# A graph layer with routed experts on one core: edge sums split into two single products, earlier residuals and routing, denser expert blocks

## The chip, the core and the metric

The kernel runs on one core of a Trainium2 chip. The core has five engines that each work through their own list of instructions in order: TensorE (PE in the profile, its weight loads PEld), VectorE (DVE), ScalarE (ACT), GpSimd (POOL) and SyncE (SP, which here only issues transfers). They wait for each other by semaphores, and transfers go through 16 DMA engines. The metric is the device time of one execution in microseconds. Eleven runs of the kernel before gave a median of 1468.36 us (1464.17 to 1476.13).

## What is computed

A layer over 6250 nodes of 256 values (x) and 100000 edges (src, dst, weight), with dst sorted. In short:

```python
xn = layernorm(x)
h = xn @ W;  deg = segment_sum(edge_weight, dst) + 1;  dinv = rsqrt(deg)
agg = segment_sum(dinv[src] * edge_weight * dinv[dst] * h[src], dst) + dinv**2 * h
g = relu(0.5 * (layernorm(agg + b) * gamma + beta) + 0.5 * xn)
q, k = elu(xn @ Wq.T) + 1, elu(xn @ Wk.T) + 1;  v = xn @ Wv.T        # 8 heads of 32
x1 = x + g + (q @ (k.T @ v) / max(q . k.sum, 1e-6)) @ Wproj.T + bproj
y = layernorm(x1);  logits = y @ gate_w + gate_b                      # 16 experts, the best 2
moe = sum over the best 2 of softmax weight * (relu(y @ w1[e] + b1[e]) @ w2[e] + b2[e])
out = x1 + layernorm(y + moe) * gamma2 + beta2
```

## The kernel before, in words

Nodes lie in 49 tiles of 128 rows (X stays in SBUF). Edges lie in 782 chunks of 128; eight chunks form a group g, and a group's destinations lie in a window of 128 rows at steps of 64, so that two or three groups fill a tile.

**Setup** (to about 100 us): edge lists are transposed into columns (`columns`), degrees are summed on TensorE from one-hot factors that VectorE builds (L448, L452, L460), the row statistics are taken, and the table `w_hs` of rows dinv * xn is written to DRAM from Q, seven tiles at a time (`table`, L519 to L531).

**Main loop** (L1300): a slot is one chunk. In slot c GpSimd gathers the chunk's 128 table rows from DRAM into one of 12 row buffers (L1306), and VectorE builds a 128x128 matrix `hot` of edge weights at the edges' destinations (L1310). LAG = 6 slots later TensorE multiplies hot by the rows in float32 and adds into the group's accumulator (L1319); each such product is recorded as two matmuls. A finished group is scaled and added to its tile's sum `agg` (L1331). PE, DVE, ACT and SP execute exactly the order in which the program is written; GpSimd's instructions alone are placed by the scheduler.

Everything else is woven into slots by `Weave`: a piece of work is a generator that is put at a slot, and each `yield n` lets n slots go by. `attend` (a tile each 3.6 slots up to slot 157) makes queries into Q and the attention's sums. `residual` (two tiles at a time, at slot 16 * t1 + 4 + LAG + 3 or later, ten slots apart) turns sums into x1, takes its statistics, normalises it on ScalarE (L745), transposes and copies it, and multiplies by gate_w (L754) for the logits, 22 slots in all. For each of eleven phases of tiles (PHASES: up to tile 8, 12, 16, ... 40, 46, 49) `route` comes RES = 24 slots behind the last residual; it takes the best two experts and gives each token a place in blocks of 128 tokens of one expert (slot_i, L906). `scatter` normalises the phase's tiles on ScalarE (L994) into four places and writes the rows by GpSimd to `w_xslots` (L1005); a fifth tile's activation waits until a scatter has left its place. `expert` loads a block's weights (about 1.1 MB) and tokens by SP, four blocks deep, and needs TensorE for two transposes (L1076), w1 (L1087) and w2 (L1098). Blocks stand seven slots apart, six in the phase that ends at tile 40, four behind that or near the end. `combine` gathers each token's two results (L1145) and writes the output.

The transfers that clear w_xslots and w_yslots (1 MB each) stand on SP's queue: 11 during setup, 23 from slot 4 on.

The slots of interest: phase 9 (tiles 40 to 45) is routed at slot 773; the last two residuals start at 781 and 791; the last phase is routed at 815; 78 of 114 blocks start at or before slot 782; block 88, the first of the last phase, starts at 829.

## Time and profile before

| what | value |
|---|---|
| median of 11 runs | 1468.36 us |
| profiled execution: time, span | 1469.18 us, 1467.4 us |
| mean granted TensorE clock | 0.936 |
| first and last gather of the main loop start | 104.5 us, 1207.4 us |
| first transposes of block 88 | 1289.7 us |
| first and last gather of combine start | 1291.2 us, 1447.9 us |

A line of the profile's groups gives the source line, engine, operation, what it writes and reads, the count, then busy time in us and mean ns of one, then the idle time of the engine just before and what ended most of it. A line of the timeline gives start, duration, engine, line and operation, with idle time and releaser in brackets. A line of the stretches gives the stretch, its length, then for PE, PEld, DVE, ACT and POOL the busy us (and number of instructions), then the granted clock, the DMA engines' share and GB/s. A stretch's DMA share and an engine's busy time are of that stretch alone, so they say more than the shares of the whole span.

### The profile page before, as it was taken

The numbers are of one execution on the slowest core, as the hardware profiler recorded it, in microseconds if no ns is written. First come the engines' busy times: TensorE is split into PE (matmuls) and PEld (weight loads), VectorE is DVE, ScalarE is ACT, GpSimd is POOL, SyncE is SP. The second block draws the span as 40 slices with busy tenths as digits, with TensorE's granted clock in tenths as the row PEclk, the third lists the DMA queues.
The fourth block names the chain that finished last, engine by engine and source line by source line (L and its number), as shares of the span: only waits on it lengthen the run. The fifth ranks groups of instructions, "written<-read, shape, count | busy, mean of one in ns | idle before, by whom it ended". The sixth has DMA issues, their size and how long they took to land. (4 is left out here: it accounts for less than half of the span.)

```text
span 1467.4 us, 24332 instructions
## 1 busy us (share of the span) xinstructions
PE 1230.8 (84%) x6923; PEld 994.8 (68%) x6923; DVE 953.9 (65%) x3302; ACT 500.6 (34%) x1354; POOL 961.2 (66%) x999
## 2 busy tenths in 40 slices
PE   4879999978777788979889798798988997968890
PEld 3846666646655677868678687686877886857770
DVE  7954454458877484756847568375684666568885
ACT  3763444422322222313223232232332233434551
POOL 1017777777767777777777777777777773167643
PEclk9999999999967999999999999898998998989995
DMA  8979943333335777778768687786767886989993
GB/s 257 317 261 371 382 134 102 105 104 113 110 104 168 230 251 265 254 232 265 266 230 299 228 261 244 259 270 224 268 212 267 294 290 219 314 291 385 376 325 93
DMA packets 176921, 353.83 MB, mean 241 GB/s; under 512 B 26769, under 2 KB 116020, under 8 KB 176770
## 3 DMA queue, kind: packets, MB, share of 16 engines
q1 hardware_dynamic: 128790, 223.10, 44.1%
q0 software_dynamic: 47712, 128.17, 27.6%
q8 instruction: 61, 1.00, 0.3%
q10 hardware_dynamic: 268, 0.82, 0.2%
q14 instruction: 90, 0.74, 0.2%
HBM read 277.60 MB, written 74.38 MB: 240 GB/s over the span
## 5 line engine op out<-in xcount | busy, mean ns | idle before, releaser
L1306 POOL DMA_INDIRECT rows<-w_hs,src_t x782 | 754.7, 965 | 329.2 <-issue 92.3
L1319 PE MATMUL acc<-rows,hot 128*128 128x256 f32 x1564 | 446.3, 401 | 91.4 <-DMA rows<-w_hs,src_t 78.9
L1310 DVE TENSOR_SCALAR hot<-iota_g,loc_t,w_t 128x128 f32<-128x128 f32 x782 | 268.6, 361 | 285.0 <-PE acc L1319 278.7
L1319 PEld LDWEIGHTS acc<-rows,hot 128*128 128x128 f32 x1564 | 278.3, 198 | 168.4 <-issue 72.4
L1005 POOL DMA_INDIRECT w_xslots<-Q,slot_i x98 | 100.5, 1025 | 80.5 <-ACT Q L1081 41.0
L1098 PE MATMUL yp<-early,hT 128*128 128x256 f32 x592 | 144.5, 388 | 1.0 <-ACT hT L1094 0.8
L1145 POOL DMA_INDIRECT Q<-w_yslots,slot_i x98 | 100.1, 1021 | 66.1 <-DVE xn L1161 22.9
L1094 ACT ACTIVATE hT<-hp,early 128x128 f32<-128x128 f32 x296 | 84.3, 368 | 149.9 <-PE hp L1087 115.3
L1087 PE MATMUL hp<-Q,early 128*128 128x128 f32 x992 | 125.3, 281 | 8.0 <-ACT Q L1081 8.0
L1087 PEld LDWEIGHTS hp<-Q,early 128*128 128x128 f32 x992 | 122.1, 196 | 13.3 <-ACT Q L1081 10.3
L1098 PEld LDWEIGHTS yp<-early,hT 128*128 128x128 f32 x592 | 114.0, 196 | 18.0 <-ACT hT L1094 2.2
L1081 ACT COPY Q<-xtp 128x256 f32<-128x256 f32 x114 | 42.2, 370 | 225.5 <-PE xtp L1076 223.2
L1087 PE MATMUL hp<-Q 128*128 128x128 f32 x832 | 111.3, 291 | 8.8 <-ACT Q L1081 8.8
L1087 PEld LDWEIGHTS hp<-Q 128*128 128x128 f32 x832 | 108.1, 206 | 13.6 <-ACT Q L1081 11.4
L576 PE MATMUL kq<-early,xnT 128*128 128x512 f32 (+1 forms) x196 | 94.5, 605 | 4.1 <-ACT xnT L572 4.1
L324 ACT ACTIVATE sd<-mv,eps_t 128x2 f32<-128x2 f32 (+2 forms) x76 | 22.6, 298 | 217.9 <-DVE mv L320 212.2
L1098 PE MATMUL yp<-Q,hT 128*128 128x256 f32 x320 | 79.8, 394 | 2.3 <-ACT hT L1094 2.2
L706 PE MATMUL hp<-w_sb,two_a 128*128 128x256 f32 (+1 forms) x196 | 58.1, 449 | 19.7 <-ACT two_a L678 19.7
L1098 PEld LDWEIGHTS yp<-Q,hT 128*128 128x128 f32 x320 | 61.4, 198 | 12.7 <-ACT hT L1094 4.5
L1331 DVE SCALAR_TENSOR_TENSOR agg<-acc,dinv,agg 64x256 f32<-64x256 f32 x135 | 64.9, 481 | 2.8
L706 PEld LDWEIGHTS hp<-w_sb,two_a 128*128 128x128 f32 (+1 forms) x196 | 42.4, 223 | 30.5 <-ACT two_a L678 22.0
L1094 ACT ACTIVATE hT<-hp,Q 128x128 f32<-128x128 f32 x160 | 45.4, 368 | 45.9 <-PE hp L1087 35.5
(306 smaller groups left out, 1727.6 us busy)
## 6 DMA issues: line engine op xcount, KB each, us to landing
early<-in_experts SPq DMA_DIRECT2D x61, 642.0 KB
early<-in_experts SPq DMA_DIRECT2D x62, 512.0 KB
Q<-in_experts SPq DMA_DIRECT2D x52, 512.0 KB
Q<-in_experts SPq DMA_DIRECT2D x27, 642.0 KB
w_xslots<-zero_b SPq DMA_DIRECT2D x16, 1024.0 KB
w_yslots<-zero_b SPq DMA_DIRECT2D x16, 1024.0 KB
Q<-w_xslots SPq DMA_DIRECT2D x114, 128.0 KB
w_yslots<-Q SPq DMA_DIRECT2D x114, 128.0 KB
```

The lines of the kernel that those rows point to most:

```text
L576: nc.tensor.matmul(kq[:r], xnT[:, k, :r], wkq[:, k, :], start=(k == 0), stop=(k == 1))
L706: nc.tensor.matmul(hp[:r0, i, :], agT[:, k, i * P:i * P + r0], w_sb[:, k, :], start=(k == 0), stop=(k == 1))
L1005: i = nc.gpsimd.indirect_dma_start(out=xslots, out_offset=IndirectOffsetOnAxis(ap=slot_i[:r, t, k:k + 1], axis=0), in_=y[:r], in_offset=No ...
L1081: nc.scalar.copy(xT, tp[:, :2, :])
L1087: nc.tensor.matmul(hp[:, f, :], w1[:, c, f * P:(f + 1) * P], xT[:, c, :], start=(c == 0), stop=(c == 1))
L1094: act(hT[:, f, :], hp[:, f, :], AF.Relu, bias=b1[:, f:f + 1], scale=1.0)
L1098: nc.tensor.matmul(yp[:, :D], hT[:, f, :], w2[:, f, :], start=(f == 0), stop=(f == FJ - 1 and not as_row))
L1145: g = nc.gpsimd.indirect_dma_start(out=got[i, k]()[:r], out_offset=None, in_=yslots, in_offset=IndirectOffsetOnAxis(ap=slot_i[:r, t, k:k + ...
L1306: nc.gpsimd.indirect_dma_start(out=hrows[c], out_offset=None, in_=hs, in_offset=IndirectOffsetOnAxis(ap=src_t[:, c:c + 1], axis=0))
L1310: v.tensor_scalar(hots[c], iota_g[:, group_of(c) % 2, :], loc_t[:, c:c + 1], w_t[:, c:c + 1], op0=OP.is_equal, op1=OP.mult)
L1319: nc.tensor.matmul(accs[g], hots.pop(c), hrows.pop(c), start=begin, stop=end)
L1331: v.scalar_tensor_tensor(agg(t)[p0:p1], acc[p0:p1, :], dinv[p0:p1, t:t + 1], agg(t)[p0:p1], op0=OP.mult, op1=OP.add)
```

## The change

It consists of six parts that go together.

- The sums of 420 of the 782 chunks (groups below 24, and the odd ones from 40 on: `in_parts`) no longer multiply float32 by float32. `hot` becomes a matrix of zeros and ones (VectorE compares two chunks at once), ScalarE writes row times weight into a float32r tile `high` three slots behind the gather, VectorE writes the rest of the product into `low` one slot later, and TensorE multiplies hot by high and by low, seven slots behind the gather. The other chunks keep their float32 product, six slots behind.
- The gate's product takes the transposed x1 itself; mean and deviation come in afterwards, by the column sums of gate_w (`gsum`, made once) and two small VectorE operations. The two activations of L745 and five slots fall away.
- Residuals start at 16 * t1 + 4 + LAG - 1 with LAG = 7, three slots earlier than before; routing follows 19 slots behind and not 24. Phase 9 is routed at slot 765, the last residuals start at 778 and 788, the last phase is routed at 807, block 88 starts at 821, and 81 blocks start at or before slot 782.
- The blocks of the phase that ends at tile 40 stand five slots apart.
- Gathered rows have a ring of 15 buffers of their own, high and low five each; behind the main loop a tile `late` takes that memory. To make room Q holds 36 tiles and not 49: the last tiles of the table are staged over earlier ones, and the queries of tiles 36 to 48 go to DRAM and come back eight slots before they are used. The list of sources is turned into columns before the branch on `flag`.
- The 23 transfers that clear memory during the main loop are issued by ScalarE instead of SP.

In the built order of instructions all 18 scatters of the last two phases stand behind the last gather on GpSimd, before as after, and a gather waits for as many semaphores as before (one of them VectorE's or TensorE's).

```diff
+FR = mybir.dt.float32r
...
-LAG = 6
+LAG = 7
+SPLIT = 3
+QT = 36
+RING_ROWS, RING_PARTS = 15, 5
...
-RES = 24
+RES = 19
...
+def in_parts(g):
...
+    return g < 24 or (g >= 40 and g % 2 == 1)
...
-    rows3 = top.tile([P, 3, EW], F32, name="rows3")
-    loc_e, src_e, ew_e = rows3[:ER, 0, :], rows3[:ER, 1, :].bitcast(I32), rows3[:ER, 2, :]
...
+    src_t = top.tile([P, NCA], I32, name="src_t")
...
+        rows3 = cp.tile([P, 3, EW], F32, name="rows3")
+        loc_e, src_e, ew_e = rows3[:ER, 0, :], rows3[:ER, 1, :].bitcast(I32), rows3[:ER, 2, :]
...
+        sf = cp.tile([ER, EW], F32, name="sf")
+        nc.scalar.copy(sf, src_e)
+        columns(nc, cps, ident, sf, src_t)
...
-        windowed_layer(tc, X, rows3, ident, loc_t, w_t, **rest)
+        windowed_layer(tc, X, ident, loc_t, w_t, src_t, **rest)
...
+    w_q = dram.tile([(NT - QT) * P, D], F32, name="w_q")
...
-    def fill(a, first, end):
+    def fill(eng, a, first, end):
...
-            nc.sync.dma_start(a[s * P:(s + q) * P, :].rearrange("(p q) c -> p q c", q=q),
-                              zero[:, None, :].to_broadcast([P, q, D]))
+            eng.dma_start(a[s * P:(s + q) * P, :].rearrange("(p q) c -> p q c", q=q),
+                          zero[:, None, :].to_broadcast([P, q, D]))
...
-    for _ in fill(xslots, 0, SOON):
+    for _ in fill(nc.sync, xslots, 0, SOON):
...
-                sf = sp.tile([ER, EW], F32, name="sf")
-                nc.scalar.copy(sf, src_e)
-                columns(nc, sps, ident, sf, src_t)
...
-    Q = sums.tile([P, NT, D], F32, name="Q")
+    Q = sums.tile([P, QT, D], F32, name="Q")
...
+    staged = [t if t < 5 * TG else t - 4 * TG for t in range(NT)]
...
-        r = rows(t)
+        r, j = rows(t), staged[t]
...
-            act(Q[:r, t, :], X[:r, t, :], AF.Identity, bias=nmr[:r, t:t + 1], scale=rsd[:r, t:t + 1])
+            act(Q[:r, j, :], X[:r, t, :], AF.Identity, bias=nmr[:r, t:t + 1], scale=rsd[:r, t:t + 1])
...
-            v.tensor_scalar(Q[:r, t, :], X[:r, t, :], mv1[:r, t, 0:1], rsd[:r, t:t + 1],
+            v.tensor_scalar(Q[:r, j, :], X[:r, t, :], mv1[:r, t, 0:1], rsd[:r, t:t + 1],
...
-            nc.sync.dma_start(hs[t0 * P:(t0 + n) * P, :].rearrange("(t p) c -> p t c", p=P), Q[:, t0:t0 + n, :])
+            j = staged[t0]
+            nc.sync.dma_start(hs[t0 * P:(t0 + n) * P, :].rearrange("(t p) c -> p t c", p=P), Q[:, j:j + n, :])
...
-                nc.sync.dma_start(hs[NFULL * P:, :], Q[:rows(NFULL), NFULL, :])
+                nc.sync.dma_start(hs[NFULL * P:, :], Q[:rows(NFULL), j + n, :])
...
+    gsum = wp.tile([P, NE], F32, name="gsum")
...
-        v.scalar_tensor_tensor(Q[:r, t, :], e[:r, 1, :], 1.0, pos[:r, 1, :], op0=OP.min, op1=OP.add)
+        q = Q[:, t, :] if t < QT else mp.tile([P, 2, D], F32, name="h2", bufs=2)[:, 0, :]
+        v.scalar_tensor_tensor(q[:r], e[:r, 1, :], 1.0, pos[:r, 1, :], op0=OP.min, op1=OP.add)
...
+        if t >= QT:
+            nc.sync.dma_start(w_q[(t - QT) * P:(t - QT) * P + r, :], q[:r])
...
+        gs = bank("gs")
+        for k in range(2):
+            nc.tensor.matmul(gs[:, :NE], ones, gw[:, k, :], start=(k == 0), stop=(k == 1))
+        v.tensor_copy(gsum, gs[:, :NE])
...
-    def queries(t0):
...
-        return Q[:, t0:min(NT, t0 + 2), :]
...
+    def queries(t0):
...
+        j = t0 if t0 < QT else 9 + (t0 - QT) // 2 % 2 * 2
+        return Q[:, j:j + 2, :]
...
+    def load_queries(ts_):
...
+        for i, t in enumerate(ts_):
+            r = rows(t)
+            nc.sync.dma_start(queries(ts_[0])[:r, i, :], w_q[(t - QT) * P:(t - QT) * P + r, :])
+        return
+        yield
...
-        q = Q[:r0, t0:t1, :]
+        q = queries(t0)[:r0, :n, :]
...
+        tp = turn([X[:r0, t, :] for t in ts_])
...
+        xT = kept(tp, "yT", 1)
...
-        yield 1
-        y = []
+        rest = mp.tile([P, 2, NE], F32, name="rest", bufs=1)
...
-            y.append(mp.tile([P, D], F32, name="row", bufs=3))
-            act(y[i][:r0], X[:r0, t, :], AF.Identity, bias=nm2[:r0, t:t + 1], scale=rs2[:r0, t:t + 1])
-        yield 2
-        tp = turn([a[:r0] for a in y])
-        yield 1
-        yT = kept(tp, "yT", 1)
-        yield 2
+            v.scalar_tensor_tensor(rest[:r0, i, :], gsum[:r0], nm2[:r0, t:t + 1], gb[:r0], op0=OP.mult, op1=OP.add)
+        yield 1
...
-                nc.tensor.matmul(gl[:r0, i, :NE], yT[:, k, i * P:i * P + r0], gw[:, k, :], start=(k == 0), stop=(k == 1))
-        yield 1
-        v.tensor_tensor(logits[:r0, t0:t1, :], gl[:r0, :n, :NE], gb[:r0, None, :].to_broadcast([r0, n, NE]), op=OP.add)
+                nc.tensor.matmul(gl[:r0, i, :NE], xT[:, k, i * P:i * P + r0], gw[:, k, :], start=(k == 0), stop=(k == 1))
+        yield 1
+        for i, t in enumerate(ts_):
+            v.scalar_tensor_tensor(logits[:r0, t, :], gl[:r0, i, :NE], rs2[:r0, t:t + 1], rest[:r0, i, :], op0=OP.mult, op1=OP.add)
...
-    hrow = rows3.rearrange("p a (i d) -> p (a i) d", d=D)
-    NROW = 3 * EW // D
+    NROW = RING_ROWS + 2 * RING_PARTS
+    ringed = ExitStack()
+    rp = ringed.enter_context(tc.tile_pool(name="w_ring", bufs=1))
+    late = []
...
+    def late_row(i):
+        if not late:
+            late.append(msg.enter_context(tc.tile_pool(name="w_late", bufs=1)).tile([P, NROW, D], F32, name="late"))
+        return late[0][:, i, :]
...
+    LATE = 12
...
-        weave.add(fill_at, fill(a, first, MOST + 1))
+        weave.add(fill_at, fill(nc.scalar, a, first, MOST + 1))
...
-            at = max(at, min(NCH, 16 * t1 + 4) + LAG + 3)
+            at = max(at, min(NCH, 16 * t1 + 4) + LAG - 1)
...
+            if t0 >= QT:
+                weave.add(at - 8, load_queries(range(t0, t1)))
...
-            block = max(block + (4 if n > AFTER or block > NCH - 9 else 6 if n == AFTER else 7), ready)
+            block = max(block + (4 if n > AFTER or block > NCH - 9 else 5 if n == AFTER else 7), ready)
...
-    hrows, hots, accs = {}, {}, {}
+    hrows, highs, lows, hots, accs = {}, {}, {}, {}, {}
...
-            hrows[c] = hrow[:, c % NROW, :]
+            hrows[c] = rp.tile([P, D], F32, name="hrow", bufs=RING_ROWS)
...
-            hots[c] = mp.tile([P, P], F32, name="hot", bufs=LAG + 1)
-            v.tensor_scalar(hots[c], iota_g[:, group_of(c) % 2, :], loc_t[:, c:c + 1], w_t[:, c:c + 1],
-                            op0=OP.is_equal, op1=OP.mult)
-        c = slot - LAG
-        if 0 <= c < NCH:
+        c = slot - 3
+        if 0 <= c < NCH and c % 2 == 0:
+            full = [P, 2, P]
+            g = group_of(c)
+            if in_parts(g):
+                hot = mp.tile(full, FR, name="hot", bufs=4)
+                v.tensor_tensor(hot, iota_g[:, g % 2:g % 2 + 1, :].to_broadcast(full),
+                                loc_t[:, c:c + 2, None].to_broadcast(full), op=OP.is_equal)
+            else:
+                hot = mp.tile(full, F32, name="hot", bufs=4)
+                for i in range(2):
+                    v.tensor_scalar(hot[:, i, :], iota_g[:, g % 2, :], loc_t[:, c + i:c + i + 1], w_t[:, c + i:c + i + 1],
+                                    op0=OP.is_equal, op1=OP.mult)
+            hots[c], hots[c + 1] = hot[:, 0, :], hot[:, 1, :]
+        c = slot - SPLIT
+        if 0 <= c < NCH and in_parts(group_of(c)):
+            highs[c] = rp.tile([P, D], FR, name="high", bufs=RING_PARTS)
+            act(highs[c], hrows[c], AF.Identity, scale=w_t[:, c:c + 1])
+        c = slot - SPLIT - 1
+        if 0 <= c < NCH and in_parts(group_of(c)):
+            lows[c] = rp.tile([P, D], FR, name="low", bufs=RING_PARTS)
+            v.scalar_tensor_tensor(lows[c], hrows.pop(c), w_t[:, c:c + 1], highs[c].bitcast(F32), op0=OP.mult, op1=OP.subtract)
+        for c, parts in ((slot - LAG, True), (slot - LAG + 1, False)):
+            if not (0 <= c < NCH and in_parts(group_of(c)) == parts):
+                continue
...
-            nc.tensor.matmul(accs[g], hots.pop(c), hrows.pop(c), start=begin, stop=end)
+            hot = hots.pop(c)
+            if parts:
+                nc.tensor.matmul(accs[g], hot, highs.pop(c), start=begin, stop=False)
+                nc.tensor.matmul(accs[g], hot, lows.pop(c), start=False, stop=end)
+            else:
+                nc.tensor.matmul(accs[g], hot, hrows.pop(c), start=begin, stop=end)
...
+        if slot == NCH + LAG + 1:
+            ringed.close()
```

## The prediction

> **What bounds the kernel now.** I read the busy shares, then busy time by stretch, then GpSimd's instructions in order of time, then the end after the last gather.
>
> ```profile
> PE 1230.8 (84%) x6923; PEld 994.8 (68%) x6923; DVE 953.9 (65%) x3302; ACT 500.6 (34%) x1354; POOL 961.2 (66%) x999
> ...
> L1306 POOL DMA_INDIRECT rows<-w_hs,src_t x782 | 754.7, 965 | 329.2 <-issue 92.3
> L1319 PE MATMUL acc<-rows,hot 128*128 128x256 f32 x1564 | 446.3, 401 | 91.4 <-DMA rows<-w_hs,src_t 78.9
> ```
>
> By these shares TensorE looks like the bound. It isn't, for most of the time. A gather takes 0.95 us, and 0.30 us lies before each, whoever is named as releaser:
>
> ```profile
> 709.64 0.95 POOL L1306 DMA_INDIRECT rows<-w_hs,src_t  x1 [0.30 <-DMA rows<-w_hs,src_t]
> 710.89 1.17 POOL L1306 DMA_INDIRECT rows<-w_hs,src_t  x1 [0.30 <-PE acc L1319]
> 712.37 0.95 POOL L1306 DMA_INDIRECT rows<-w_hs,src_t  x1 [0.30 <-PE xtp L1076]
> ```
>
> From 104.5 us (first gather) to 1207.4 (last), 862 such instructions (782 gathers, 80 scatters) stand at a median pitch of 1.251 us: 861 x 1.251 = 1077 of the 1103 us. The other 26 are 5.1 us of true waits (4.04 and 1.62 before the gathers at 412 and 415 us) and 21 us of instructions longer than 0.946. So **this stage costs what GpSimd costs**; a faster TensorE buys nothing in it.
>
> Behind the last gather TensorE and the transfers take over:
>
> ```profile
> 1226.50 0.60 ACT L994 ACTIVATE Q<-X,nm,rs 128x256 f32<-128x256 f32 x1 [15.85 <-DMA w_xslots<-Q,slot_i]
> ...
> 1227.62 3.65 PE L706 MATMUL hp<-w_sb,two_a 128*128 128x256 f32 x8 [6.88 <-ACT two_a L678]
> ...
> 1289.74 0.69 PE L1076 MATMUL xtp<-ident,Q 128*128 128x128 f32 x2 [3.88 <-DMA Q<-w_xslots]
> ...
> 1290.00:1425.00 135.00, 113.67 (x673) 94.53 (x673) 114.90 (x328) 64.59 (x205) 83.09 (x82) 0.94 1.00 362
> ```
>
> Call the last gather's start T. ScalarE, which works in order, holds a row to be normalised for the scatter until an earlier scatter has left its place (T+19.1); TensorE idles 11 us of 12; then it is busy 57.5 of 58.5 us to T+78.6 and waits for block 88's tokens. Block 88 begins at T+82.3. From there to the end, 177.7 us, the DMA share is 1.00.
>
> **The change, part by part.** The profiled execution took 1469.18 us (span 1467.4); the 11 runs have a median of 1468.36, 0.8 lower.
>
> *Setup, +2.4.* The transposes of src move ahead of the branch, and VectorE's first memset behind it now waits for the last of them. w_t's copies end at 12.53; cast 1.05 (L466), eight transposes 1.57 (L152): 15.4 instead of 13.03. VectorE's run up to 39.3 us has no wait, and TensorE's degree sums (24.35 + 4.75 us, back to back) start when it delivers, so all of it moves the first gather. Bounds 0 (if the zero fills, no longer queued right behind the table's writes, give it back) to +3. Staging the last 14 table tiles over earlier ones waits for writes issued 9 us before: nothing; if that cover fails, some 3 us.
>
> *Own terms, fills, spilled queries: 0.* Fills go from SP's queue to ScalarE's, one per 8 slots. 13 tiles of queries go to DRAM and back: 26 issues of 128 KB on SP, over 600 us in which the DMA share is 0.36 to 0.78. On SP they stand ahead of block loads that are prefetched up to four deep.
>
> *Split sums.* 420 of the 782 chunks (188 with g < 24, 232 in odd groups from 40) get: a scale on ScalarE (nearest L650, 0.51 us), a subtraction on VectorE with both big operands in SBUF (nearest L728, 0.48), an is_equal per two chunks (two SBUF inputs, nearest L1177, 0.425) in place of two L1310 of 0.36, and two float32r products. No row shows such a product: between 0.21 us a pair (each like half a float32 record; ten L1319 records take 2.32 us) and 0.86 (each like a float32 product of two records). I take 0.21 to 0.43, nearest to the one bf16 product of 256 columns, L628, 0.28 alone. Either is hidden: TensorE has 12 us in 100 to spare from 500 on; only in 150 to 250 (50.00 of 50) does it need the saving.
>
> What isn't hidden is on GpSimd. A long gather and a two-input VectorE operation go together:
>
> ```profile
> 594.27 0.68 DVE L731 SCALAR_TENSOR_TENSOR X<-h,X 128x512 f32<-128x512 f32 x1
> 594.32 1.46 POOL L1306 DMA_INDIRECT rows<-w_hs,src_t  x1 [0.31 <-PE acc L1319]
> ```
>
> L731 began 0.04 before the gather and ended 0.64 after its start; the gather ended 0.82 later. Over the timeline this holds: where an operation with two large SBUF inputs (L584, L585, L688, L695, L725, L727, L728, L731) began at least 0.04 before a gather and ends more than 0.126 after its start, the gather is longer by what exceeds 0.126. The 260 gathers beside L1310 alone average 0.949; those beside L728 1.046. An operation of length L that falls anywhere costs (L-0.166)^2/2/1.251: 0.107 us for 0.68, 0.039 for 0.48, 0.026 for 0.42. Check on before: 92 + 92 + 86 such operations give 9.8 + 3.6 + 2.2 = 15.6; the gathers that meet them are 16.3 too long.
>
> The Trainium skill (SBUF — State Buffer, "Who interferes with whom") says that a VectorE instruction with two SBUF inputs contends with a GpSimd instruction that reads SBUF, and that the later one blocks for all of the other. The trace agrees on which, not on how much: only an instant near the start is exposed. By the page each of 420 subtractions could hold a gather for up to 0.48 us, +200 us, and the change would lose plainly.
>
> By the rows: the subtraction follows the landing. In the first stage a gather lands 2.46 us after its start (2.5 +- 0.15 between 206 and 400 us), its product could begin at 2.8 to 2.9 (chunks 140 to 180), the scale ends near 3.36, the subtraction runs from 3.42 to 3.90; the third gather behind starts at 3.75, so 0.02: 188 x 0.02 = 3.8. From 500 on landings spread over 3.5 +- 0.95, so any phase: 232 x 0.039 = 9.1. The is_equal: 210 x 0.0265 = 5.6. **+18.5**. Below: 0 (never met). Above: each subtraction late by the worst 0.29, which stretches three gathers at once: 0.105 x 420 = 44.
>
> *Ring of 15 rows, not 12: -4.* A gather may now run 9 slots ahead of its product instead of 6. The waits of 4.04 and 1.62 are shorter than 3 slots more (3.75) but for the first's end: about 1 of 5.1 stays. Bounds -5 to 0.
>
> *The end, -22.* Route of tiles 40 to 45 moves from slot 773 to 765, the last residuals from 781 and 791 to 778 and 788, the last route from 815 to 807, block 88 from 829 to 821; blocks 63 to 80 stand five slots apart, so block 80 starts at 776, not 793. The scatters still stand behind the last gather on GpSimd. Before, slot_i came at T+10.9, the first scatter at T+11.9; 8 slots (10 us) earlier it comes at about T+1, the scatter at T+1.3. The normalising activations then end their waits 7.2 us later, as before: T+8.5 and T+11 against T+19.1 and T+21.5. Queued behind them on ScalarE are the last scales, and on them VectorE's subtractions and TensorE's products. From T+11.5 TensorE has left: sums 2, residuals 6.3 + 3.1, routes 1.2, and 9.5 blocks at 3.73 (0.22 + 1.78 + 1.73) = 35.4; 48 us, to T+59.5 (before 59.3 us of work). The gate's product from X drops two activations (1.1 us) and five slots from each residual. The other path: last logits at T+32, route 16.5 (as from 1258.0 to 1274.7), six scatters 7, landing 6, load 2: T+63.5. I take T+60.5 for block 88, since before TensorE's path was the longer one but for 3.9 us: -22. Bounds -8 (the 8 slots alone, at 1.25, with nothing gained from fewer blocks) to -28. The 177.7 us behind block 88 stay: same bytes at a full DMA share.
>
> *Sum:* 2.4 + 18.5 - 4 - 22 = -5.1: 1464.1 beside the profiled 1469.2, 1463 beside the median.
>
> **Rivals.** A, slower: *collisions on GpSimd*. If ScalarE is regularly 0.1 to 0.3 us late, each subtraction ends just behind a gather's exposed instant: 44 + 5.6 instead of 18.5, 1463 + 31 = 1494. It decides from about 0.06 us a gather on. For it: all 420 subtractions hang on landings at fixed distance. Against: spread of landings from 500 on.
> B, slower: *ScalarE sets the pace in the first 188 slots*. It is busy 24.15 of 50 us in 200 to 250; 40 scales (16 to 20) and 5 fill issues (0.65 us on SP while its queue was free, up to 4.3 behind others) make 44 to 52, in order, and TensorE and VectorE wait for it. 10% over 235 us is +24: 1487. Against: its waits for TensorE shrink with the products.
> C: *the end gains half*, because route and scatter and not TensorE are last: 1463 + 11 = 1474.
> D: a float32r product is no cheaper than a float32 one: 0.43 us more on 188 chunks in a full stage, 81 us, and some 30 later: 1574.
>
> **How the numbers follow.** Forecast 0.56 (own range 1450 to 1470), C 0.16, A 0.13, B 0.11, D 0.04. Below 1443 would need the end's best bound and almost no collisions; above 1490 is half of A and D. A measurement can tell 0.3%, 4.4 us. Faster by more: 0.47 of the forecast's 0.56. Within: 0.09 and half of C, 0.17. Slower: A, B, D and half of C, 0.36.
>
> **What would show it.** First gather near 107. Mean gather pitch 1.25 in groups without split, 1.27 to 1.30 in those with; long gathers beside the new subtraction. Last gather near 1224; block 88's transposes some 60 us behind it, then 178 to the end. Wrong if ScalarE has no idle time before 340 us, if gathers with splits exceed 1.35, or if block 88 comes 70 us behind the last gather.

## The result and the profile after

The changed kernel takes 1517.96 us (median of 12 runs, 1510.07 to 1524.56), the kernel before 1469.41 (46 runs on the same chips): a ratio of 1.0325, interval 1.0306 to 1.0343. Forecast was 1463, range to 1490; the change is slower, and by more than the range held. One run of no_split below took 1763.0 us at a granted clock of 0.66, in a slower state, and is left out of its figures. The profiled execution has a span of 1518.6 us against 1467.4. The 51.2 us between them come apart by the prediction's own stages (in brackets what it gave):

| stage | before | after | difference |
|---|---|---|---|
| first gather | 104.5 | 106.4 | +1.9 (+2.4) |
| GpSimd instructions beyond 0.946 us each, to the last gather | 21.1 | 50.3 | +29.2 (+18.5) |
| true waits before gathers | 5.1 | 19.9 | +14.8 (-4) |
| last gather to the end | 260.0 | 265.1 | +5.1 (-22) |

Here and below a true wait is the part beyond 0.31 us of the gap between two GpSimd instructions. The page of the changed kernel, busy shares and then the groups that the split brings:

```profile
PE 1202.4 (79%) x6927; PEld 980.7 (65%) x6927; DVE 1074.9 (71%) x3586; ACT 645.2 (42%) x1725; POOL 990.3 (65%) x998
...
L1340 POOL DMA_INDIRECT hrow<-w_hs,src_t x782 | 784.8, 1004 | 344.1 <-issue 88.0
L1360 ACT ACTIVATE high<-hrow,w_t 128x256 fp32r<-128x256 f32 x420 | 202.5, 507 | 248.9 <-DMA hrow<-w_hs,src_t 177.3
L1364 DVE SCALAR_TENSOR_TENSOR low<-hrow,w_t,high 128x256 fp32r<-128x256 f32 x420 | 198.3, 480 | 142.5 <-ACT high L1360 136.1
L1378 PE MATMUL acc<-hrow,hot 128*128 128x256 f32 x724 | 215.6, 415 | 40.4 <-DMA hrow<-w_hs,src_t 34.8
...
L1375 PE MATMUL acc<-high,hot 128*128 128x256 f32 x420 | 155.1, 386 | 3.9 <-ACT high L1360 3.9
...
L1376 PE MATMUL acc<-low,hot 128*128 128x256 f32 x420 | 119.0, 299 | 25.5 <-DVE low L1364 24.0
```

A gather is 1004 ns long in the mean instead of 965: 30 us over 782. A float32r product is one record, where a float32 product is two (L1378 has 724 for 362 chunks); TensorE's busy time fell by 28 us, in a stage that it does not bound. VectorE's rose by 121.

What a held gather looks like, in the timeline of all engines:

```profile
194.20 0.42 DVE L1349 TENSOR_TENSOR hot<-iota_g,loc_t 128x256 fp32r<-128x256 f32 x1
...
194.53 0.48 DVE L1364 SCALAR_TENSOR_TENSOR low<-hrow,w_t,high 128x256 fp32r<-128x256 f32 x1
...
194.62 1.22 POOL L1340 DMA_INDIRECT hrow<-w_hs,src_t  x1 [0.30 <-DVE hot L1349]
```

The subtraction ends 0.39 after the gather's start, and the gather takes 1.22 instead of 0.95: 0.27 more, which is 0.39 less 0.126. Here the prediction's rule holds. At 15 places of the changed kernel, and none of the kernel before, an instruction of GpSimd is held for longer than the rule says. One of them:

```profile
229.73 0.87 DVE L1364 SCALAR_TENSOR_TENSOR low<-hrow,w_t,high 128x256 fp32r<-128x256 f32 x2
...
230.21 1.54 POOL L1340 DMA_INDIRECT hrow<-w_hs,src_t  x1 [0.30 <-DVE low L1364]
...
230.53 0.41 DVE L1349 TENSOR_TENSOR hot<-iota_g,loc_t 128x256 fp32r<-128x256 f32 x1
```

The second subtraction ends 0.39 after the gather's start, the is_equal right behind it 0.73 after. The gather is 0.59 too long: 0.73 less 0.126 is 0.60, so its length fits the end of the second operation and not of the first.

Of the 19.9 us of waits 18.7 lie between 377 and 437 us. First TensorE's timeline ahead of the longest wait, then this wait on GpSimd, then what the transposes at L696 waited for over the run:

```profile
420.68 0.81 PE L1378 MATMUL acc<-hrow,hot 128*128 128x256 f32 x3
428.04 1.12 PE L696 MATMUL tp<-ident,X 128*128 128x128 f32 x4 [6.55 <-DVE X L757]
428.94 1.06 PE L696 MATMUL tp<-ident,agg 128*128 128x128 f32 x4
429.80 1.91 PE L1378 MATMUL acc<-hrow,hot 128*128 128x256 f32 x4
```

```profile
431.13 0.94 POOL L1340 DMA_INDIRECT hrow<-w_hs,src_t  x1 [5.85 <-PE acc L1378]
```

```profile
its engine sat idle before it (us, times) until:
  DVE X L757: 80.9, 23
```

Nothing ran on TensorE for 6.55 us: next in its written order stood the gate's transposes of X, and VectorE had not added X yet. The products stood behind them, and the gathers wait for a row of the ring that a product must give back. Over the run TensorE sat 80.9 us at this place; only a part of it reached the gathers.

Then the end, in ScalarE's timeline; T is again the last gather's start, 1253.5:

```profile
1257.45 0.51 ACT L1360 ACTIVATE high<-hrow,w_t 128x256 fp32r<-128x256 f32 x1
1267.83 0.60 ACT L1016 ACTIVATE Q<-X,nm,rs 128x256 f32<-128x256 f32 x1 [9.87 <-DMA w_xslots<-Q,slot_i]
...
1273.06 0.58 ACT L703 COPY two_a<-tp 128x512 f32<-128x512 f32 x1
```

TensorE by stretches of 10 us (columns: busy TensorE, weight load, VectorE, ScalarE, GpSimd, then granted clock, DMA share, GB/s), and block 88's first transposes:

```profile
1263.50:1273.50 10.00, 5.76 (x26) 4.38 (x24) 5.97 (x26) 5.67 (x15) 7.61 (x8) 0.67 0.59 218
...
1293.50:1303.50 10.00, 8.05 (x25) 5.70 (x25) 4.65 (x15) 1.42 (x5) 0.00 (x0) 0.67 0.47 160
```

```profile
1338.44 0.69 PE L1098 MATMUL xtp<-ident,Q 128*128 128x128 f32 x2 [5.09 <-DMA Q<-w_xslots]
```

The normalising activation's wait ends at T+14.3 (T+19.1 before). The copy two_a of the second last residual, which stands behind it, comes at T+19.6, as it did before (1227.01, T+19.6), because the last scales of the split, the next residual activations and a block's now stand between the two. So nothing of the sooner route reached the residual. Block 88 begins at T+84.9, not T+60.5, and 180.2 us follow. Up to there TensorE runs ten blocks behind the last gather, against thirteen before, and is busy for 68.3 us, against 66.7.

### The profile page after: what moved, and what is told of

Read it like the earlier page. It is cut to its first block, busy times and chain, and to the rows that moved or that the text cites. A ratio compares the mean times of both kernels' runs of the same rounds, so it can differ in the third digit from the quotient of the medians.

```text
span 1518.6 us, 25306 instructions
## 1 busy us (share of the span) xinstructions
PE 1202.4 (79%) x6927; PEld 980.7 (65%) x6927; DVE 1074.9 (71%) x3586; ACT 645.2 (42%) x1725; POOL 990.3 (65%) x998
## 5 line engine op out<-in xcount | busy, mean ns | idle before, releaser
L1340 POOL DMA_INDIRECT hrow<-w_hs,src_t x782 | 784.8, 1004 | 344.1 <-issue 88.0
L1360 ACT ACTIVATE high<-hrow,w_t 128x256 fp32r<-128x256 f32 x420 | 202.5, 507 | 248.9 <-DMA hrow<-w_hs,src_t 177.3
L1364 DVE SCALAR_TENSOR_TENSOR low<-hrow,w_t,high 128x256 fp32r<-128x256 f32 x420 | 198.3, 480 | 142.5 <-ACT high L1360 136.1
L1378 PE MATMUL acc<-hrow,hot 128*128 128x256 f32 x724 | 215.6, 415 | 40.4 <-DMA hrow<-w_hs,src_t 34.8
L1378 PEld LDWEIGHTS acc<-hrow,hot 128*128 128x128 f32 x724 | 133.2, 206 | 65.5 <-DMA hrow<-w_hs,src_t 20.5
L1375 PE MATMUL acc<-high,hot 128*128 128x256 f32 x420 | 155.1, 386 | 3.9 <-ACT high L1360 3.9
L1167 POOL DMA_INDIRECT late<-w_yslots,slot_i x98 | 99.6, 1017 | 69.7 <-DVE xn L1183 39.5
L1376 PE MATMUL acc<-low,hot 128*128 128x256 f32 x420 | 119.0, 299 | 25.5 <-DVE low L1364 24.0
L1120 PEld LDWEIGHTS yp<-early,hT 128*128 128x128 f32 x592 | 115.3, 201 | 32.2 <-ACT hT L1116 16.5
L1376 PEld LDWEIGHTS acc<-low,hot 128*128 128x128 f32 x420 | 83.6, 199 | 44.9 <-DVE low L1364 35.5
L1354 DVE TENSOR_SCALAR hot<-iota_g,loc_t,w_t 128x128 f32<-128x128 f32 x362 | 109.0, 353 | 0.0
L1390 DVE SCALAR_TENSOR_TENSOR agg<-acc,dinv,agg 64x256 f32<-64x256 f32 x135 | 64.9, 481 | 35.7 <-PE acc L1378 19.1
```

Of the source, the lines that this page charges most:

```text
L1120: nc.tensor.matmul(yp[:, :D], hT[:, f, :], w2[:, f, :], start=(f == 0), stop=(f == FJ - 1 and not as_row))
L1167: g = nc.gpsimd.indirect_dma_start(out=got[i, k]()[:r], out_offset=None, in_=yslots, in_offset=IndirectOffsetOnAxis(ap=slot_i[:r, t, k:k + ...
L1340: nc.gpsimd.indirect_dma_start(out=hrows[c], out_offset=None, in_=hs, in_offset=IndirectOffsetOnAxis(ap=src_t[:, c:c + 1], axis=0))
L1354: v.tensor_scalar(hot[:, i, :], iota_g[:, g % 2, :], loc_t[:, c + i:c + i + 1], w_t[:, c + i:c + i + 1], op0=OP.is_equal, op1=OP.mult)
L1360: act(highs[c], hrows[c], AF.Identity, scale=w_t[:, c:c + 1])
L1364: v.scalar_tensor_tensor(lows[c], hrows.pop(c), w_t[:, c:c + 1], highs[c].bitcast(F32), op0=OP.mult, op1=OP.subtract)
```

## The experiments

Unless said otherwise a run is the changed kernel with one edit, and its ratio is against the kernel before on the same chip.

**no_split.** The sums as before.

```diff
-    return g < 24 or (g >= 40 and g % 2 == 1)
+    return False
```

> The changed kernel without the split sums: all 782 chunks get the float32 product, the rest of the change stays. Theory 1 (two-input VectorE operations of the split hold the gathers): the excess of GpSimd's instructions over 0.946 us falls from 50 us to 22 to 26 and the last gather comes 25 us sooner or more. Theory 2 (the waits before gathers, 20 us in the changed kernel, come from the gate's transposes and the sooner residuals, not from the split): they stay at 15 to 20, and the time is 1518 - 27 = 1491. Rival (they come from the longer chain scale, subtraction, product): they fall to 5, and the time is 1476. Third possibility: float32 products fill TensorE again in the first 250 us and the waits grow there; then 1500 or more.

1484.5 us (median of four), ratio 1.0085 (1.004 to 1.013). Instruction excess 29.0 instead of 50.3, waits 16.7 instead of 19.9, end 255.2 instead of 265.1. The time lies between theory 2's 1491 and the rival's 1476 and doesn't decide; the waits do, for theory 2. The split pays for 21 us of instructions and some 3 of the waits. That the end comes 10 us sooner had not been expected, and the excess stayed 3 us above its range.

**old_gate.** Gate's product from the norm again, routes 24 slots behind.

```diff
-RES = 19
+RES = 24
...
-        tp = turn([X[:r0, t, :] for t in ts_])
...
+            act(y[i][:r0], X[:r0, t, :], AF.Identity, bias=nm2[:r0, t:t + 1], scale=rs2[:r0, t:t + 1])
+        yield 2
+        tp = turn([a[:r0] for a in y])
...
```

> The changed kernel with the gate's product taken from the norm again (normalising activations, then transposes; routes five slots later, as before). Theory (the transposes of X stand on TensorE's queue ahead of VectorE's addition of X, and the chunks' products queue behind them): waits before gathers fall from 20 us to about 5 and the time to 1503 to 1508 (some of the gain given back by routes that begin five slots later). Rival (the waits come from residuals begun three slots sooner, or from VectorE being late for any instruction): waits stay at 15 to 20, time 1518 to 1525.

1504.8 us, ratio 1.0222 (1.0181 to 1.0263). Waits 11.8, neither 5 nor 15 to 20; the time fits the theory. The gate's transposes make some 8 us of the waits, not all 15.

**late_turn.** Only the place of these transposes.

```diff
-        tp = turn([X[:r0, t, :] for t in ts_])
         for i, t in enumerate(ts_):
             stats(mp, mv2[:r0, t, :], X[:r0, t, :])
+        yield 2
+        tp = turn([X[:r0, t, :] for t in ts_])
         yield 1
```

> The changed kernel with the gate's four transposes of X written two slots later, behind the statistics, and the steps behind them two slots later; no other difference. Theory (the transposes reach TensorE before X is ready): waits before gathers fall from 20 us to 5 to 8, 1505 or so. Rival (residuals begun sooner, VectorE late in any case): waits stay above 14 us, 1515 to 1522.

1499.2 us, ratio 1.0183 (1.0135 to 1.0231): 19 us less than the changed kernel, by two slots more in each residual. Waits 10.6, last gather 1241.3, end 254.5. What the transposes waited for, in this kernel:

```profile
its engine sat idle before it (us, times) until:
  DVE X L757: 14.7, 13
```

80.9 us of TensorE's idle time have become 14.7. Between the two profiled executions lie 22.8 us: 9.3 of waits, as the theory said but not as far (5 to 8), 4.9 of instruction excess and 10.6 at the end, neither of which had been expected, less 1.9 of a later first gather.

**six_slots.** 

```diff
-            block = max(block + (4 if n > AFTER or block > NCH - 9 else 5 if n == AFTER else 7), ready)
+            block = max(block + (4 if n > AFTER or block > NCH - 9 else 6 if n == AFTER else 7), ready)
```

> The changed kernel with the blocks behind tile 40 six slots apart again. If the end is set by TensorE's work behind the last gather: three blocks more there, 3 x 3.7 = 11 us, 1529. If it is set by the chain last residual, logits, route, scatter, load: 1518 plus or minus 3, and the stretch from the last gather to the end stays at 265.

1515.1 us, ratio 1.0291 (1.0257 to 1.0326): no slower than with five. The profile has the stretch to the end at 255.8 and the last gather 5 us later. It is a weaker test than was meant: TensorE runs 11 blocks between the last gather and block 88 instead of 10, not three more. It shows something else. Here slot_i came at T-1.8, the first scatter at T+1.3, and the hold on ScalarE ended at T+7.9, all as early as the prediction had them or earlier; the last products by gate_w (L775) still came at T+43.6 and block 88 at T+77.1.

**split_alone.** The split stays, and all else that orders the work is undone: old_gate's edit and six_slots', and

```diff
-            at = max(at, min(NCH, 16 * t1 + 4) + LAG - 1)
+            at = max(at, min(NCH, 16 * t1 + 4) + LAG + 2)
```

> The changed kernel with everything but the split undone that orders the work: gate's product from the norm, routes 24 slots behind, residuals three slots later (nine behind the sums, as before), six slots between blocks; ring of 15 rows, fills and spilled queries stay. Theory (the split alone costs 25 us on GpSimd, the waits of the changed kernel come from gate and residuals): instruction excess 45 to 50, waits before gathers 3 to 6, end 258 to 262, 1469 + 2 + 25 = 1496 (1490 to 1500). Rival (the split is harmless without the sooner residuals): 1471 to 1478.

1502.6 us, ratio 1.0226 (1.0187 to 1.0264). Instruction excess 45.5, end 262.0, both as the theory said; waits 9.0 instead of 3 to 6, the time 2.6 us above its range. The split is the larger half of the loss, and needs neither the gate nor the sooner residuals nor the denser blocks for it; ring, fills and spilled queries were still there.

**extra_two, extra_one, extra_stats: the hold by itself.** The kernel before with one more VectorE operation per chunk of g >= 40, 466 in all:

```diff
+        c = slot - 4
+        if 0 <= c < NCH and group_of(c) >= 40:
+            v.tensor_tensor(hrows[c], hrows[c], hrows[c], op=OP.max)
```

and in its place `v.tensor_scalar(hrows[c], hrows[c], 1.0, 0.0, op0=OP.mult, op1=OP.add)`, or `v.bn_stats(st, hrows[c])`.

> The kernel before, with one more VectorE operation on each gathered row of the 466 chunks with g >= 40: the maximum of the row with itself, in place, two big SBUF inputs, about 0.42 us; the result is the same. Theory (such an operation holds a gather that starts while it runs): at any phase 0.026 us each, by the mean of the subtraction in the changed kernel 0.030, so the excess of GpSimd's instructions rises from 21 us by 12 to 14 and the time to about 1482 (1478 to 1486). By the Trainium skill (SBUF — State Buffer, "Who interferes with whom", the later of the two is held for all of the other) it could be up to 0.42 each, 196 us. Rival (no lock; VectorE's 195 us more of work make what it feeds late): excess stays at 21, and extra_one takes as long as this.

> The kernel before, with one more VectorE operation on the same 466 rows that has one big SBUF input (times 1, plus 0, in place, about 0.41 us). Theory: excess of GpSimd's instructions stays at 21 to 23 us, time 1469 plus or minus 4. Rival (VectorE's extra work counts, whatever its inputs): as extra_two.

> extra_stats again (466 more VectorE operations of one SBUF input, 0.42 us, not of the fast form), beside a kernel before of 1469 us. Theory (only a second input or the fast form holds a gather): instruction excess 21 to 26 us, time 1469 to 1475. Rival: excess 33 or more.

| operation | inputs in SBUF | mean, ns | excess, us | over 21.1, per operation | time, ratio |
|---|---|---|---|---|---|
| maximum (extra_two) | two | 419 | 53.6 | 0.070 | 1499.8, 1.0215 (1.0181 to 1.0248) |
| times 1 plus 0 (extra_one) | one | 307 | 33.3 | 0.026 | 1481.1, 1.0072 (1.005 to 1.0095) |
| statistics (extra_stats_2) | one | 419 | 27.2 | 0.013 | 1474.0, 1.0035 (1.0008 to 1.0062) |

The first and the third keep VectorE equally long and differ by 26 us on GpSimd: the hold is real, and it goes by the operation, not by VectorE's load. But the maximum costs 0.070 and not 0.026 to 0.030; that the multiplication, with one input, would be free was wrong; and the third missed its range of excess by 1 us. The multiplication takes 0.28 us alone, less than the other two, and while it runs it holds a gather too. Two instances, from the timelines of extra_two and extra_one:

```profile
567.90 0.42 DVE L1314 TENSOR_TENSOR rows<-rows 128x256 f32<-128x256 f32 x1 [0.84 <-DMA rows<-w_hs,src_t]
567.96 1.18 POOL L1306 DMA_INDIRECT rows<-w_hs,src_t  x1 [0.30 <-DMA rows<-w_hs,src_t]
```

```profile
1165.16 0.28 DVE L1314 TENSOR_SCALAR rows<-rows 128x256 f32<-128x256 f32 x1
1165.19 1.07 POOL L1306 DMA_INDIRECT rows<-w_hs,src_t  x1 [0.30 <-PE acc L1322]
```

0.36 less 0.126 is 0.23 (1.18 less 0.95); 0.25 less 0.126 is 0.12 (1.07 less 0.95). The Trainium skill (SBUF — State Buffer, "Who interferes with whom") names both kinds as contending with GpSimd: two SBUF inputs, and a tensor_scalar in a two-port mode. The runs agree on the kinds, batch-norm statistics being free or nearly; that the multiplication ran in such a mode is read from its 0.28 us, not shown. On the size they do not agree: a hold costs what is left of VectorE's work at one instant of the gather, in the mean 0.070 for the maximum, where the whole operation would be 0.42.

**no_low.** The scale and the is_equal stay; subtraction and second product of the split groups go, so their sums lack the rounded-off part of the rows.

```diff
-            act(highs[c], hrows[c], AF.Identity, scale=w_t[:, c:c + 1])
+            act(highs[c], hrows.pop(c), AF.Identity, scale=w_t[:, c:c + 1])
...
-            v.scalar_tensor_tensor(lows[c], hrows.pop(c), w_t[:, c:c + 1], highs[c].bitcast(F32), op0=OP.mult, op1=OP.subtract)
...
-                nc.tensor.matmul(accs[g], hot, highs.pop(c), start=begin, stop=False)
-                nc.tensor.matmul(accs[g], hot, lows.pop(c), start=False, stop=end)
+                nc.tensor.matmul(accs[g], hot, highs.pop(c), start=begin, stop=end)
```

> no_low again (the changed kernel without subtraction and second product of the split groups, which leaves out the rounded-off part of the rows in their sums), beside a kernel before of 1469 us. Theory (the subtraction holds the gathers): instruction excess falls from 50 us to 27 to 32, waits stay at 15 to 20, 1493 to 1499. Rival (scale and is_equal carry the loss): excess above 40, 1508 or more.

1490.4 us, ratio 1.0166 (1.0135 to 1.0198). Instruction excess 24.9, waits 16.5, end 259.6. Without the subtraction (and the second product) 25.4 of the 29.2 us are gone. The 3.8 that stay are not the price of the scales and the is_equal alone, since the matrices that the is_equal replaces are gone too: with these, made two at a time, no_split has an excess of 29.0.

**gate_alone.** From the other side: the kernel before with the gate's product from X, its transposes placed as in late_turn, and RES = 21; nothing else of the change.

> gate_alone again, beside a kernel before of 1469 us. Theory: waits before gathers 5 to 9 us, instruction excess 20 to 25 us, last gather 1207 to 1212, stretch to the end 253 to 257: 1460 to 1467. Rival: 1468 to 1473.

1462.3 us, ratio 0.9961 (0.9945 to 0.9977). Waits 0.0 (better than expected), excess 21.7, last gather 1204.0, end 256.6. This part is worth some 6 us by itself.

**no_split_later.** The whole change without the split, with late_turn's edit, residuals three slots later and RES = 21.

> The changed kernel without the split, with the gate's transposes of X two slots later and the residuals three slots later; routes 21 slots behind the residuals. Theory: waits before gathers 5 to 8 us, instruction excess 26, last gather near 1217, end 250 to 256: 1467 to 1473, about as before; if the five slots that the gate saves reach the end, down to 1460. Rival (the waits come from the ring, the fills or the spilled queries): waits stay at 15, 1478 or more.

1472.0 us, ratio 1.0016 (0.9998 to 1.0034): some ten us behind gate_alone (eight by the ratios), which has the same gate and the same distance of residuals from their sums. First gather 2.5 us later, waits 5.3 against 0.0, instruction excess 30.9 against 21.7, end 253.6 against 256.6. So what is left (matrices of weights made two at a time and three slots behind the gather, setup, longer ring, fills on ScalarE's queue, spilled queries, five slots) costs some 8 to 10 us. Which of it was not separated.

**six_places.** ScalarE's hold at the end. gate_alone with six places in SBUF for the normalised tiles 40 to 45 instead of four:

```diff
-        weave.add(ready + 2, scatter(n, a, b, 9, "token" if slow else "got", slow))
+        weave.add(ready + 2, scatter(n, a, b, 9, "token" if slow and n <= AFTER else "got", slow))
```

> gate_alone with one line more: the six normalised tiles 40 to 45 that are scattered behind the last gather get six places in SBUF (of those for the results of blocks, free by then) instead of four, so that no normalising activation waits on ScalarE until an earlier scatter has left its place; the number and order of all other instructions stay. Theory (this hold on ScalarE, to 14 to 19 us behind the last gather, is what keeps the last residual's logits at 50 us): logits of the last tile at 36 to 42 us, last scatter at 54 to 60, the stretch to the end 244 to 251, time 8 to 14 us below gate_alone, 1450 to 1458. Rival (TensorE's blocks in their written order, at a lower clock, keep the logits at 45 to 50): no faster than gate_alone.

1453.9 us, ratio 0.9914 (0.9889 to 0.9938): 8.5 us below gate_alone and faster than both kernels of this case. ScalarE's timeline behind the last gather, in gate_alone (T = 1204.0) and in this kernel (T = 1200.2):

```profile
1216.89 0.60 ACT L997 ACTIVATE Q<-X,nm,rs 128x256 f32<-128x256 f32 x1 [13.89 <-DMA w_xslots<-Q,slot_i]
...
1219.15 0.60 ACT L683 COPY two_a<-tp 128x512 f32<-128x512 f32 x1
```

```profile
1208.47 0.58 ACT L683 COPY two_a<-tp 128x512 f32<-128x512 f32 x1 [5.02 <-PE tp L676]
```

The hold of 13.9 us is gone and two_a comes at T+8.3 instead of T+15.2; the last products by gate_w come at T+39.7 instead of T+45.1. The rival, TensorE's written order, had no such gain. The stretch to the end is 251.5, just outside what was expected, and 5.1 us shorter than gate_alone's. The other 3.8 us between the two profiles lie ahead of the last gather, in the first gather's start (1.9) and the excess (1.9), which the edit doesn't touch: 5 us is the safer figure.

**On another chip.** gate_alone, no_low, extra_stats and after_again (the changed kernel unaltered) were first run on a chip where the kernel before itself took 1718.6 us and gathers waited 225 to 337 us; these runs are compared with one another only.

> The kernel before with one part of the change alone: gate's product from X (transposes of X two slots behind the statistics' place in the changed kernel's late variant), routes 21 slots behind the residuals instead of 24. Ring of 12 rows, residuals nine slots behind their sums, fills and setup as before. Theory (this part is what is good in the change): first gather at 104, waits before gathers 5 to 9 us, instruction excess 21 to 25, stretch from the last gather to the end 253 to 257 instead of 260: 1462 to 1468. Rival (nothing reaches the end): 1468 to 1473.

> The changed kernel without the subtraction and without the second product of the split groups: it leaves out the rounded-off part of the rows in their sums. Theory (the subtraction holds the gathers): instruction excess falls from 50 us to 27 to 32, waits before gathers stay at 15 to 20, last gather 20 to 25 us sooner, time 1493 to 1499. Rival (the scale and the is_equal carry the loss): excess stays above 40, 1508 or more.

> The kernel before with one more VectorE operation on each row of the 466 chunks with g >= 40, one SBUF input and not of the fast form of extra_one (batch-norm statistics of the row, about 0.42 us as in extra_two, written to six numbers nobody reads). Theory (only a second input or the fast form holds a gather): instruction excess 21 to 26 us, time 1469 to 1475. Rival (any VectorE work beside a gather holds it, or VectorE's longer queue does): excess 33 or more, as extra_one (33) or extra_two (54).

> The changed kernel unaltered, for a second profile beside six_slots, whose stretch from the last gather to the end was 256 us against 265 here. Theory (the granted clock behind the last gather sets most of that difference): 253 to 258 if the clock stays at 0.95 or more from 20 to 60 us behind the last gather, 262 to 267 if it falls to 0.75 or less there. Rival (five slots against six do): 262 to 267 at any clock.

Ratios 0.9954 (0.9922 to 0.9985), 1.064 (1.0571 to 1.0708), 1.0028 (0.9997 to 1.006) and 1.0495 (1.043 to 1.056). gate_alone gains there too, and extra_stats costs 0.3%, which is within the noise here (0.35% above). no_low has an instruction excess of 24.4 against 32.6 of the changed kernel, and is slower than it all the same: in that regime the waits decide, not the holds. after_again's stretch of 279.5 us can't be set beside 265.1, since from block 88 on alone it took 199.8 us instead of 180.2. Up to block 88 the same TensorE work took 60.5 us instead of 68.3, at a mean granted clock of 0.91 instead of 0.83, and block 88 came at T+79.7 instead of T+84.9. So the clock may be some 5 of the 9 us between the changed kernel's end and six_slots'; on another chip this is a hint, and the expectation stays undecided.

## Why the prediction was wrong, step by step

*What bounds the kernel:* right. GpSimd sets the pace up to the last gather, 28 us less of TensorE bought nothing, and the stages add up to the loss.

*Setup, +2.4:* +1.9 between the two profiles. Over all the profiles (the other chip left out) the first gather starts at 100.7 to 105.5 us with the old setup and at 106.2 to 108.3 with the new one, medians 4.0 apart; so the upper bound of +3 was too low, and the agreement of the two profiles is in part luck.

*Split sums, +18.5:* right mechanism, wrong size: +29.2. The failed step is the price of one operation by itself, "An operation of length L that falls anywhere costs (L-0.166)^2/2/1.251", from which "232 x 0.039 = 9.1" and the is_equal's 5.6 are made. Here is the excess of GpSimd's instructions, in us, by the VectorE operation whose end fits the instruction's length to 25 ns:

| held by | before | after | extra_two |
|---|---|---|---|
| a two-input operation (both large, in SBUF) begun 0.04 us or more ahead of the start: the rule's case | 12.7 | 27.7 | 23.2 |
| one begun later, up to 0.10 behind the start | 0.5 | 4.4 | 9.5 |
| one operation and then others right behind it | 0 | 11.0 | 13.8 |
| the rest | 7.9 | 7.2 | 7.1 |

The rule's own case grew by 15.0 us, less than the 18.5 given (in extra_two by 10.5, where 12 to 14 were expected). The two others were put at nothing and grew by 14.9. Both belong to a VectorE with work queued. Of the two-input operations begun between 0.04 before and 0.10 behind an instruction's start, none of 61 that came after a pause held it, in before, after and extra_two together; of those right behind another operation 12 of 52 did in the changed kernel and 30 of 71 in extra_two. The change itself filled the queue: VectorE is busy 121 us longer. That the queue is the reason is read from these counts; no run varied it alone. Nor is it known what lets a gather go: at 83 places of the changed kernel a second two-input operation stood right behind the first, and the gather was free at the end of the first all the same.

Taking the subtraction out took 25.4 us away, 0.060 for each of 420, where the rule gave it 12.9. The is_equal was put at 5.6; in no_low's trace its operations hold 31 gathers, for 4.8 us. The upper bound of 44 held. Rival A, collisions on GpSimd, has the direction and less than its price, but its reason isn't shown: it expected them in the first 188 chunks, where 9.1 of the 29.2 us lie; 17.8 lie from chunk 316 on.

*ScalarE, rival B, and float32r, rival D:* neither. ScalarE was busy 30 to 36 of 50 us between 100 and 300 us, and a pair of float32r products took 0.32 us back to back (median of 339), in the middle of the guess of 0.21 to 0.43.

*Ring, -4:* wrong in sign of the whole: waits grew to 19.9. The step took the waits of before for a matter of ring depth alone. Some 8 to 9 of the 14.8 new ones come from TensorE's written order. Moving the gate's transposes up to X was costed as "drops two activations (1.1 us) and five slots from each residual", with no word on what TensorE then waits for. By the runs: late_turn takes 9 of the 19.9 away, old_gate 8; split_alone has 9.0, and gate_alone with the short ring 0.0. What makes the 10.6 that late_turn still has, with the longer ring, was not found.

*End, -22:* wrong; +5. The failed step is "From T+11.5 TensorE has left ... 48 us, to T+59.5", and with it the other path's "last logits at T+32". (The sum also took T+60.5 where its own other path ended at T+63.5; with that it would have been -19.) In the table T is each run's own last gather; the last gate products are TensorE's last by gate_w, the blocks and the busy time those between T and block 88, the scatters the first of the last six; no_low and gate_alone are the runs beside a kernel before of 1468 us.

| kernel | blocks | TensorE busy, us | last gate products, T+ | last six scatters, T+ | block 88, T+ | end, T+ |
|---|---|---|---|---|---|---|
| before | 13 | 66.7 | 50.0 | 67.3 | 82.3 | 260.0 |
| after | 10 | 68.3 | 50.2 | 68.7 | 84.9 | 265.1 |
| split_alone | 13 | 69.0 | 51.4 | 68.8 | 85.1 | 262.0 |
| old_gate | 11 | 65.0 | 49.4 | 68.1 | 83.8 | 262.7 |
| no_low | 10 | 62.5 | 46.8 | 64.1 | 79.6 | 259.6 |
| no_split | 10 | 63.0 | 45.3 | 62.6 | 77.8 | 255.2 |
| late_turn | 10 | 60.7 | 46.6 | 60.6 | 76.3 | 254.5 |
| six_slots | 11 | 62.1 | 43.6 | 60.9 | 77.1 | 255.8 |
| gate_alone | 12 | 65.0 | 45.1 | 62.3 | 78.8 | 256.6 |
| no_split_later | 11 | 63.5 | 41.3 | 58.5 | 73.7 | 253.6 |
| six_places | 12 | 63.2 | 39.7 | 57.0 | 73.0 | 251.5 |

From the scatters to the end it is 192.6 to 196.4 us in all of them, and block 88 waits 3.9 to 5.3 us for its tokens: the chain of gate products, route and scatters comes last. The number of blocks left does not order the runs: ten blocks stand beside T+76.3 and beside T+84.9.

The prediction saw ScalarE's hold and that the last scales are queued behind it; it let the hold end at T+8.5 (measured 14.3; the first scatter came at T+6.4 and not T+1.3) and the residual follow at once. Behind the hold stood the scales, then the copy two_a, at T+19.6 as ever. But the hold is only part of it. In six_slots it ended at T+7.9 and in six_places there was none, and from two_a to the last gate products 30 and 31.5 us passed there too (27 to 32 in every row but no_split_later's 23.1). The prediction left 20.5, from T+11.5 to T+32. In TensorE's written order two to five blocks stand between the steps of the two last residuals.

And TensorE, with gaps meanwhile, had a granted clock of 0.67 to 0.72 in four of the five stretches from T+10 to T+60 (before: 0.67, 0.82, then 1.00), where a block's sixteen products took up to 3.6 us instead of 1.95; "busy 48 us" was reckoned at full clock. So three blocks fewer than before kept it busy longer. late_turn runs the same ten blocks in 60.7 us instead of 68.3, at a mean clock of 0.93 instead of 0.83 up to block 88: 7.6 of the 8.6 us by which its block 88 comes sooner. Why the clock was lower in the changed kernel no run shows; it is one profile.

*Fills, own terms, spilled queries at 0:* not confirmed. no_split_later stands 8 to 10 us behind gate_alone, and these are among what differs.

The condition "block 88 comes 70 us behind the last gather" was named as what would make the forecast wrong, and it came: 84.9.

## What to carry to other kernels

When a queue of GpSimd's indirect DMAs sets the pace, price each VectorE operation that is added by its kind (two SBUF inputs, or the fast one-input form) and by how full VectorE's queue is, and test the price with a dummy operation before building on it. An instruction that is moved up in an in-order queue is not free: look up when its operand is ready, and what is queued behind it. Work left behind a milestone sets the end only if the last dependency chain is shorter; here two places more in SBUF for waiting activations brought the end some 5 us forward, and all the work that was moved, in the changed kernel, brought it none.

## What was not expected of the hardware

Most gathers that were held up were held for what remained of one VectorE operation beyond 0.126 us after their start, mostly to within 20 ns, whether the operation was 0.28, 0.42 or 0.48 us long. Some of GpSimd's instructions, 15 in the changed kernel and 20 in extra_two, stayed held through further operations that stood right behind it, for up to 1.85 us. A one-input multiplication of 128x256 in 0.28 us held a gather; batch-norm statistics of the same row in 0.42 us added 0.013 us a gather at most. An operation begun as late as 0.1 us after the gather's start could still hold it if it stood right behind another VectorE operation, and did not in any of 61 cases if VectorE had paused. And one of the chips ran every kernel 17 to 23% longer, with 225 to 337 us of waits before gathers while the 4096-byte packets of GpSimd's queue took a mean of 208 ns on the first chip and 209 on that one, in the changed kernel's two profiles; the reason wasn't found.
